# Self products of a block pair as seven partial products of 256 columns, and a run-end table from one-pass products, in a two-layer graph network kernel

## The chip, the cores and the metric

The kernel runs on one core of a Trainium2 chip. The metric is the device time of one execution in microseconds (us); the times given are of single executions and their median. A profile is one execution recorded by the hardware profiler. TensorE's records are called PE (matmuls) and PEld (weight loads), VectorE's DVE, ScalarE's ACT, GpSimd's POOL; SP is the engine that issues most plain DMAs.

## What is computed

There are 10,000 nodes with 512 features each and 160,000 edges, sorted by destination, each of one of four types.

```python
# layer 0, h = relu(layernorm(x))
h_all = einsum('nd,rdf->nrf', h, rel_W) + rel_b          # four relations
agg   = segment_sum(h_all[src, edge_type], dst) / max(deg, 1)
x1    = layernorm(h + h @ self_W + self_b + agg)
x     = x + layernorm(x1 + gelu(x1 @ W1 + b1) @ W2 + b2)
# layer 1, h = relu(layernorm(x)): twice
h     = relu(h @ W_self + (segment_sum(h[src], dst) / max(deg, 1)) @ W_neigh + b)
x     = x + h
```

All is fp32. The tables that say where each node's edges begin and end are made by the kernel too, from `dst`.

## The kernel before

**Two programs in one.** The first stage makes the table of messages (`hall_d`, 10,000 rows of four times 512) and the self terms (`xs_d`), and beside it the edge tables. Then three stages gather message rows and sum them per node, with the dense layers between. The first stage is ordered by a scheduler over the whole of it; the later stages stand in the order in which they are written. A branch between them takes a general program instead, where the edges do not fit the tables; it is not taken with these inputs.

**The table stage.** Nodes go in 78 blocks of 128 rows and a last one of 16. Blocks are taken in pairs (`sets`): first the block of 16, then 39 pairs. For a pair, `opened` normalises the rows, `turned` applies relu on ScalarE (`hg`, L641) and transposes each block by four products with the identity (`pT`, L172; copied out by ScalarE, L173). `mixed` (L651) forms four sums `s` of quarters of the transposed pair.

**Seven products for eight.** A pair of blocks by two halves of the contraction, times two relations' weights, is a 2 by 2 by 2 block product. The kernel forms it from seven products with sums before and after (the Winograd form). With `j` = 0 and 1 it does relations 0 and 2, then 1 and 3. Each of a half step's seven products (`times`, L724) is two matmuls of 128 by 128 by 512, into a PSUM tile `pm` from a pool of four buffers, `psM`. VectorE reads each with an addition (L731 to L748), and two additions in SBUF (L738, L739) finish the sums. Four stores per half step write `hall_d` from SP.

**The self product.** `residual`, once per half step, adds `ln2b` to the block's input rows (L657) and forms one block's self product: four matmuls of 512 columns with `wself` (L664) into a `pm` tile, which VectorE reads with the bias into `hg` (L666). `wself` has the identity added at the start (L682), which is the `h +` of the reference. `stored` writes the pair to `xs_d` (and its input rows to `xr_d`). The 12 pairs with blocks 52 to 75 (`late`) form no self product here: they store the transposed rows in `hT_d`, and a later stage does the product (L926). So 27 pairs and the block of 16 do it in the table stage.

**The edge tables.** `edges` is a generator; from the second pair on, each half step takes one of its steps with `next(step)`. `runs` finds the ends of the runs of equal destinations. Edges lie 1,250 to a partition; a key per run end holds its position, and twelve rounds of "eight largest, then strike them out" (L242, L245) take the ends out. Then, in twelve rounds of eight ends per partition, VectorE makes one-hot rows of the block (`inb`, L282) and of the lane (`inl`, L286), multiplies the latter by the edge number `end_f` (L289), and eight matmuls per round sum their products into one PSUM tile `pn` (L292): a table of the last edge number per node. What follows (L298 on) takes running maxima, degrees and offsets, on 79 partitions. `lists` then reads windows of the edge records (`win`, gathered by GpSimd) and makes the gather rows (`picked`, L468 to L491, and others). Both took their scratch from one pool `ep2` with two buffers a name.

**The start.** Weight differences (`mixes`, L704 to L707) are made by VectorE as the relation weights arrive. The small constants of the edge tables (L321 to L349) are put there too by the scheduler.

Of the kernel before, what the change touches and what calls it, by code (L numbers as in the profile page):

```python
# [21 lines left out]
def kernel(  # L22
# [152 lines left out]
    def runs(ep, ep2, pse, found):  # L175
# [15 lines left out]
        for p, n in ((0, P - 16), (P - 16, 15)):  # L191
# [11 lines left out]
        nc.gpsimd.iota(iota_j, pattern=[[1, EC]], base=1, channel_multiplier=0,  # L203
                       allow_small_or_imprecise_dtypes=True)
        base_e = ep.tile([P, 1], F32, name="base_e")
        nc.gpsimd.iota(base_e, pattern=[[0, 1]], base=0, channel_multiplier=EC,
                       allow_small_or_imprecise_dtypes=True)
        yield
        d_n = ep.tile([P, EC + 1], F32, name="d_n")
# [45 lines left out]
        n8 = ROUNDS * 8  # L255
        top_i = ep.tile([P, n8], I32, name="top_i")
        to_i = ep.tile([P, n8], I32, name="to_i")
        end_f = ep.tile([P, n8], F32, name="end_f")
        to_f = ep.tile([P, n8], F32, name="to_f")
        blk_f = ep.tile([P, n8], F32, name="blk_f")  # L260
        real = ep.tile([P, n8], F32, name="real")
        nc.vector.tensor_copy(top_i, top)
        nc.vector.tensor_scalar(to_i, top_i, 11, None, op0=OP.arith_shift_right)
        nc.vector.tensor_scalar(top_i, top_i, 2047, None, op0=OP.bitwise_and)
        nc.vector.tensor_copy(end_f, top_i)
        nc.vector.tensor_scalar(end_f, end_f, base_e, None, op0=OP.add)
        nc.vector.tensor_scalar(real, top, 0.0, sound, op0=OP.is_gt, op1=OP.mult)
        nc.vector.tensor_tensor(end_f, end_f, real, op=OP.mult)
        nc.vector.tensor_scalar(to_f, to_i, d_f[:, 0:1], None, op0=OP.add)
        nc.vector.tensor_copy(to_i, to_f)  # L270
        nc.vector.tensor_scalar(top_i, to_i, 7, None, op0=OP.arith_shift_right)
# [7 lines left out]
        for i in range(ROUNDS):  # L279
            w = slice(8 * i, 8 * i + 8)  # L280
            inb = ep2.tile([P, 8, NB], F32, name="inb")
            nc.vector.tensor_tensor(inb, lane[:, None, :NB].to_broadcast([P, 8, NB]),  # L282
                                    blk_f[:, w].unsqueeze(2).to_broadcast([P, 8, NB]),
                                    op=OP.is_equal)
            inl = ep2.tile([P, 8, P], F32, name="inl")
            nc.vector.tensor_tensor(inl, lane[:, None, :].to_broadcast([P, 8, P]),  # L286
                                    to_f[:, w].unsqueeze(2).to_broadcast([P, 8, P]),
                                    op=OP.is_equal)
            nc.vector.tensor_tensor(inl, inl, end_f[:, w].unsqueeze(2).to_broadcast([P, 8, P]),  # L289
                                    op=OP.mult)  # L290
            for j in range(8):
                nc.tensor.matmul(pn[:NB, :P], inb[:, j, :], inl[:, j, :], start=(i + j == 0),  # L292
                                 stop=(i == ROUNDS - 1 and j == 7))
            if i % 2:
                yield

        eb = ep.tile([NB, P], F32, name="eb")
        nc.vector.tensor_copy(eb, pn[:NB, :P])  # L298
        run = ep.tile([NB, P], F32, name="run")
        nc.vector.tensor_tensor_scan(run, eb, eb, 0.0, op0=OP.max, op1=OP.max)  # L300
        pr = pse.tile([P, 512], F32, name="pe")
# [278 lines left out]
            look_up(*ahead.pop(0))  # L580
            yield

    def edges(ep, ep2, pse):
        found = {k: ep.tile([P, NB], F32, name=f"f_{k}") 
                 for k in ["first", "deg", "from", "upto"] + [
                     f"{k}{lv}" for lv in range(NL) for k in ("sfrom", "supto", "sbase")]}
        with ExitStack() as s:
            yield from runs(s.enter_context(tc.tile_pool(name="er", bufs=1)), ep2, pse, found)
        with ExitStack() as s:
            yield from lists(s.enter_context(tc.tile_pool(name="el", bufs=1)), ep2, pse, found)  # L590


    with ExitStack() as s:
# [5 lines left out]
        psM = s.enter_context(tc.tile_pool(name="psM", bufs=4, space=PSUM))  # L599

        ep = s.enter_context(tc.tile_pool(name="ep", bufs=1))
        ep2 = s.enter_context(tc.tile_pool(name="ep2", bufs=2))
        step = edges(ep, ep2, pse)
        KH = KC // 2
        RH = R // 2
        sets = groups[len(groups) - (N % P > 0):] + [
# [22 lines left out]
        def opened(i):  # L629

            b0, nb, r = sets[i]
            xg = xgs.pop(i)
            sc = norm_scales(ap_, [xg[:r, c, :] for c in range(nb)], r, "a")
            return xg, sc, xp.tile([P, 2, D], F32, name="hg"), ap_.tile([P, 2, KC, P], F32,
                                                                       name="hT")
# [9 lines left out]
        def mixed(hT):  # L645

            s_ = [ap_.tile([P, KH, P], F32, name=f"s{i}", bufs=1) for i in range(4)]
            a11, a12, a21, a22 = hT[:, 0, :KH], hT[:, 0, KH:], hT[:, 1, :KH], hT[:, 1, KH:]
            for o, p, q, op in ((0, a21, a22, OP.add), (1, s_[0], a11, OP.subtract),
                                (3, a12, s_[1], OP.subtract), (2, a11, a21, OP.subtract)):  # L650
                nc.vector.tensor_tensor(s_[o], p, q, op=op)  # L651
            return a11, a12, a22, *s_

        def residual(rows, r, c, b):
            xg, _, hg, hT = rows
            h = hg[:r, c, :]
            nc.vector.tensor_tensor(xg[:r, c, :], xg[:r, c, :], ln2b[:r], op=OP.add)  # L657
            if b in late:
                i = late.index(b)
                nc.sync.dma_start(hT_d[i * P:(i + 1) * P, :], hT[:, c].rearrange("p k n -> p (k n)"))  # L660
                return
            pm = psM.tile([P, D], F32, name="pm")
            for k in range(KC):
                nc.tensor.matmul(pm[:r], rows[3][:, c, k, :r], wself[:, k, :], start=(k == 0),  # L664
                                 stop=(k == KC - 1))
            nc.vector.tensor_tensor(h, pm[:r], bself[:r], op=OP.add)  # L666
# [33 lines left out]
        for j in range(RH):  # L700
            b11, b21 = wrel[j][:, :KH], wrel[j][:, KH:]
            b12, b22 = wrel[j + RH][:, :KH], wrel[j + RH][:, KH:]
            t1, t2, t4 = (wp.tile([P, KH, D], F32, name=f"mix{j}_{i}") for i in range(3))
            nc.vector.tensor_tensor(t1, b12, b11, op=OP.subtract)  # L704
            nc.vector.tensor_tensor(t2, b22, t1, op=OP.subtract)
            nc.vector.tensor_tensor(t4, b21, t2, op=OP.subtract)
            nc.vector.tensor_tensor(b12, b22, b12, op=OP.subtract)  # L707
            mixes.append((b11, b21, b22, t1, t2, b12, t4))
        rows = opened(1)
        for c in range(2):  # L710
            turned(1, rows, c)
        for i, g in enumerate(sets):
            if g[2] < P:
                continue
            b0, nb, _ = g
            later = i + 1 if i + 1 < len(sets) else None
            if later:
                xgs[later] = load(sets[later])
            a11, a12, a22, s1, s2, s3, s4 = mixed(rows[3])

            def times(a, w):
                pm = psM.tile([P, D], F32, name="pm")
                for k in range(KH):
                    nc.tensor.matmul(pm, a[:, k, :], w[:, k, :], start=(k == 0),  # L724
                                     stop=(k == KH - 1))
                return pm

            for j in range(RH):
                b11, b21, b22, t1, t2, t3, t4 = mixes[j]
                p1, u2, p5, u3 = (ap_.tile([P, D], F32, name=n) for n in ("p1", "u2", "p5", "u3"))  # L730
                nc.vector.tensor_tensor(p1, times(a11, b11), bias(j), op=OP.add)  # L731
                nc.vector.tensor_tensor(u2, times(s2, t2), p1, op=OP.add)
                nc.vector.tensor_tensor(p5, times(s1, t1), bias(j + RH), op=OP.add)
                nc.vector.tensor_tensor(u3, times(s3, t3), u2, op=OP.add)
                gate[:] = [u3[:, :1]]
                nc.vector.tensor_tensor(p1, times(a12, b21), p1, op=OP.add)
                message(b0, j, p1)
                nc.vector.tensor_tensor(u2, p5, u2, op=OP.add)  # L738
                nc.vector.tensor_tensor(p5, p5, u3, op=OP.add)  # L739
                message(b0 + 1, j + RH, p5)  # L740
                if j == 0 and later:
                    rows_next = opened(later)
                if later:
                    residual(rows, P, j, b0 + j)
                    turned(later, rows_next, j)
                nc.vector.tensor_tensor(u3, times(a22, t4), u3, op=OP.add)
                message(b0 + 1, j, u3)
                nc.vector.tensor_tensor(u2, times(s4, b22), u2, op=OP.add)  # L748
                message(b0, j + RH, u2)
                if i > 1:  # L750
                    next(step, None)
            if not later:
                for c in range(2):
                    residual(rows, P, c, b0 + c)
            stored(g, rows)
            if later:
                rows = rows_next
# [789 lines left out]
```

## Time and profile before

| | us |
|---|---|
| runs shown | 6247.69, 6250.86, 6256.69 |
| median | 6250.86 |
| profiled execution | 6253.56 |
| its span | 6251.8 |

| engine | busy us | share of the span |
|---|---|---|
| PE | 5699.4 | 91% |
| PEld | 2517.3 | 40% |
| DVE | 3597.1 | 58% |
| ACT | 1858.2 | 30% |
| POOL | 3762.9 | 60% |

Shares of the whole span are means over stages with different limits, so the stage has to be looked at by itself: the table stage ends at about 1,236 us. The page gives the span in 40 slices of 156 us, each digit the busy share in tenths. Further views give busy time in stretches of chosen length, the chain of work that ended last (each piece followed back to what released it), and groups of equal instructions with their count, mean duration and the idle time before them. A fp32 matmul shows as two records. [...]

### The profile page before, as it was taken

What the parts mean: (1) busy time and instruction counts of PE and PEld (TensorE: products, weight loads), DVE (VectorE), ACT (ScalarE), POOL (GpSimd) and SP (SyncE); (2) the same over time, 40 slices, a digit from 0 to 9 for tenths busy, and PEclk for the clock granted to TensorE, in tenths of its full rate; (3) what the DMA queues carried; (4) which work ended last, traced back from release to release, by engine and by line L of the source; (5) the groups of instructions that cost most, each with busy time, mean ns of one, the idle gap of its engine ahead of it and who ended that gap; (6) DMA issues with size and microseconds to landing.
All of it is one profiled execution on the core that took longest, in us unless ns stands there. A gap on an engine that the chain in (4) does not pass through costs nothing.

```text
span 6251.8 us, 54551 instructions
## 1 busy us (share of the span) xinstructions
PE 5699.4 (91%) x14875; PEld 2517.3 (40%) x14875; DVE 3597.1 (58%) x7253; ACT 1858.2 (30%) x3672; POOL 3762.9 (60%) x3927
## 2 busy tenths in 40 slices
PE   9999999989999999999788888888879888888888
PEld 3444444444444444444333333333333333333333
DVE  8768889557777777776344444344334444444444
ACT  1016565013333333333322222222222222222221
POOL 0001110057777777775477777777767777777776
PEclk9999999989999999999899999999999999999999
DMA  4333344387887878886577777777778788878877
GB/s 162 114 117 118 122 136 154 132 275 243 255 256 242 256 246 252 256 257 196 187 234 237 237 234 237 237 234 237 237 232 251 249 247 251 250 246 251 250 246 217
DMA packets 503498, 1373.74 MB, mean 220 GB/s; under 512 B 82206, under 2 KB 82206, under 8 KB 503054
## 3 DMA queue, kind: packets, MB, share of 16 engines
q0 software_dynamic: 308768, 1008.91, 54.0%
q1 hardware_dynamic: 193886, 360.20, 15.9%
q8 instruction: 120, 1.97, 0.1%
q14 instruction: 196, 1.61, 0.1%
q10 hardware_dynamic: 528, 1.05, 0.1%
HBM read 1156.54 MB, written 213.30 MB: 219 GB/s over the span
## 4 chain that ended last, share of the span: by engine, by line
DMA 40%; PE 39%; DVE 8%; issue 7%; POOL 5%; ACT 1%; POOLq 0%; SPq 0%; DVEq 0%; ACTq 0%
DMA rows<-h_d,row 19%; PE pm L724 15%; DMA rows<-h_d,orow 14%; PE pa L847 6%; POOL rows L794 5%; PE ph L975 5%; PE po L986 4%; DVE pa L858 4%; DMA rows<-hall_d,row 4%; PE pm L664 3%; PE po L1218 1%; PE po L926 1%; DVE st L1013 1%; PE pT L172 1%; DMA tail<-h_d,srow 1%
## 5 line engine op out<-in xcount | busy, mean ns | idle before, releaser
L858 DVE TENSOR_TENSOR pa<-pa,rows 128x512 f32<-128x512 f32 x2574 | 1799.3, 699 | 2061.3 <-PE pa L847 1241.3
L794 POOL DMA_INDIRECT rows<-h_d,row x1716 | 1622.2, 945 | 522.7 <-issue 291.2
L847 PE MATMUL pa<-rows,hot 128*128 128x512 f32 (+1 forms) x2358 | 1247.7, 644 | 371.4 <-DMA rows<-h_d,orow 314.2
L794 POOL DMA_INDIRECT rows<-hall_d,row x858 | 868.1, 1012 | 273.6 <-issue 109.0
L794 POOL DMA_INDIRECT rows<-h_d,orow x786 | 743.1, 945 | 354.4 <-DMA h_d<-h 99.0
L847 PEld LDWEIGHTS pa<-rows,hot 128*128 128x128 f32 (+1 forms) x2358 | 407.1, 194 | 1151.9 <-DMA rows<-h_d,orow 829.0
L794 POOL DMA_INDIRECT rows<-hall_d,orow x393 | 378.2, 962 | 346.0 <-DVE hg L666 202.2
L986 PE MATMUL po<-w2s,hid 128*128 128x512 f32 (+1 forms) x1264 | 566.6, 602 | 17.2 <-DVE rest L1042 14.0
L1218 PE MATMUL po<-wss,hTb 128*128 128x512 f32 (+1 forms) x1264 | 579.7, 602 | 0.0
L1189 PE MATMUL po<-wns,mTb 128*128 128x512 f32 (+1 forms) x1264 | 573.5, 597 | 1.4 <-ACT mTb L173 1.4
L975 PE MATMUL ph<-x1T,w1s 128*128 128x512 f32 (+2 forms) x1344 | 558.7, 568 | 4.8 <-ACT hid L977 4.8
L173 ACT COPY mTb<-pT 128x512 f32<-128x512 f32 (+1 forms) x158 | 91.8, 581 | 1233.5 <-PE pT L172 1233.5
L1214 ACT ACTIVATE mb<-pa,rdeg 128x512 f32<-128x512 f32 (+1 forms) x158 | 108.5, 687 | 1130.0 <-DVE pa L858 1127.8
L829 PE MATMUL pa<-wss,ident 128*128 128x512 f32 x936 | 427.5, 593 | 0.0
L508 POOL DMA_INDIRECT win<-rec_d,at x79 | 76.0, 962 | 545.9 <-PE pe L533 364.8
L1189 PEld LDWEIGHTS po<-wns,mTb 128*128 128x128 f32 (+1 forms) x1264 | 240.2, 190 | 308.4 <-issue 272.4
L975 PEld LDWEIGHTS ph<-x1T,w1s 128*128 128x128 f32 x1344 | 249.4, 192 | 282.0 <-issue 273.4
L986 PEld LDWEIGHTS po<-w2s,hid 128*128 128x128 f32 (+1 forms) x1264 | 237.6, 191 | 308.2 <-issue 283.4
L847 PE MATMUL pa<-tail,hot 128*128 128x512 f32 x624 | 308.1, 611 | 50.6 <-DMA tail<-h_d,srow 47.1
L816 ACT ACTIVATE hot<-lane,loc 128x128 f32<-128x128 f32 x1098 | 337.7, 391 | 0.0
L1218 PEld LDWEIGHTS po<-wss,hTb 128*128 128x128 f32 (+1 forms) x1264 | 233.5, 195 | 235.3 <-issue 234.9
L724 PE MATMUL pm<-wrel,hT 128*128 128x512 f32 x624 | 296.5, 597 | 0.0
(289 smaller groups left out, 6224.5 us busy)
## 6 DMA issues: line engine op xcount, KB each, us to landing
hall_d<-p SPq DMA_DIRECT2D x156, 256.0 KB, 2.5
hall_d<-u SPq DMA_DIRECT2D x156, 256.0 KB, 2.4
hb<-h_d SPq DMA_DIRECT2D x156, 256.0 KB, 4.3
rows<-h_d,row POOLq DMA_INDIRECT x1716, 3.8
xg<-in_x_dram SPq DMA_DIRECT2D x39, 512.0 KB, 3.6
xr_d<-xg SPq DMA_DIRECT2D x39, 512.0 KB, 3.0
xs<-xs_d SPq DMA_DIRECT2D x39, 512.0 KB, 7.6
h_d<-h SPq DMA_DIRECT2D x39, 512.0 KB, 4.5
```

The costliest lines, as they stand in the source:

```text
L664: nc.tensor.matmul(pm[:r], rows[3][:, c, k, :r], wself[:, k, :], start=(k == 0), stop=(k == KC - 1))
L724: nc.tensor.matmul(pm, a[:, k, :], w[:, k, :], start=(k == 0), stop=(k == KH - 1))
L794: nc.gpsimd.indirect_dma_start(out=t[:n], out_offset=None, in_=table, in_offset=bass.IndirectOffsetOnAxis(ap=idx, axis=0))
L816: nc.scalar.activation(hot[:, t, :], lane, AF.Abs, bias=loc[:, b, t:t + 1], scale=-1.0)
L829: nc.tensor.matmul(p, ident, w, start=True, stop=True)
L847: nc.tensor.matmul(pa[:r], h, v, start=(i == 0), stop=(i == len(work) - 1))
L858: nc.vector.tensor_tensor(pa[:r], pa[:r], t[:r], op=OP.add)
L975: nc.tensor.matmul(ph[:, :n], w1s[:, k, f * P:(f + 1) * P], self.xT[:, k, :n], start=(k == 0), stop=(k == KC - 1))
L986: nc.tensor.matmul(po[:r], self.hid[:, f, c * r:(c + 1) * r], w2s[:, f, :], start=(f == 0), stop=(f == FC - 1))
L1189: nc.tensor.matmul(po[:r], mT[:, k, :r], wns[:, k, :], start=False, stop=(k == KC - 1))
L1214: nc.scalar.activation(m[:r], pa[:r], AF.Copy, scale=rdeg[:r, b:b + 1])
L1218: nc.tensor.matmul(po[:r], hT[:, k, :r], wss[:, k, :], start=(k == 0), stop=False)
```

## The change

The self products of a pair are formed like the relation products: a 2 by 2 by 2 block product over the pair's two blocks, two halves of the contraction and the two halves of 256 columns of `wself`. The sums `s` of the transposed pair, which are there already, serve again. The weight differences are made once, at the start (`halves`). The first four products are formed where block 0's self product stood, the other three where block 1's stood. The sums are kept in `hg`. Pairs in `late` and the block of 16 are as before.

In the run-end table, `end_f` holds two numbers per end: the position in its partition (1 to 1,250) and the partition's number, where one number held the partition times 1,250 plus the position. Both are multiplied with the one-hot lane row (`both`, one buffer), and one matmul of 256 columns in the reduced fp32 kind (`F32R`) sums both tables. VectorE puts them together afterwards. `inl` has one buffer, and the two halves of the edge work have scratch pools of their own.

```diff
@@ base_e
-        nc.gpsimd.iota(base_e, pattern=[[0, 1]], base=0, channel_multiplier=EC,
+        nc.gpsimd.iota(base_e, pattern=[[0, 1]], base=0, channel_multiplier=1,
...
-        end_f = ep.tile([P, n8], F32, name="end_f")
+        end_f = ep.tile([P, n8, 2], F32, name="end_f")
...
-        nc.vector.tensor_copy(end_f, top_i)
-        nc.vector.tensor_scalar(end_f, end_f, base_e, None, op0=OP.add)
+        nc.vector.tensor_copy(end_f[:, :, 0], top_i)
         nc.vector.tensor_scalar(real, top, 0.0, sound, op0=OP.is_gt, op1=OP.mult)
-        nc.vector.tensor_tensor(end_f, end_f, real, op=OP.mult)
+        nc.vector.tensor_tensor(end_f[:, :, 0], end_f[:, :, 0], real, op=OP.mult)
+        nc.vector.tensor_scalar(end_f[:, :, 1], real, base_e, None, op0=OP.mult)
@@ for i in range(ROUNDS)
-            nc.vector.tensor_tensor(inb, lane[:, None, :NB].to_broadcast([P, 8, NB]),
+            nc.vector.tensor_tensor(inb.bitcast(F32R), lane[:, None, :NB].to_broadcast([P, 8, NB]),
...
-            inl = ep2.tile([P, 8, P], F32, name="inl")
+            inl = ep2.tile([P, 8, P], F32, name="inl", bufs=1)
...
-            nc.vector.tensor_tensor(inl, inl, end_f[:, w].unsqueeze(2).to_broadcast([P, 8, P]),
+            both = ep2.tile([P, 8, 2, P], F32, name="both", bufs=1)
+            nc.vector.tensor_tensor(both.bitcast(F32R),
+                                    inl[:, :, None, :].to_broadcast([P, 8, 2, P]),
+                                    end_f[:, w].unsqueeze(3).to_broadcast([P, 8, 2, P]),
                                     op=OP.mult)
             for j in range(8):
-                nc.tensor.matmul(pn[:NB, :P], inb[:, j, :], inl[:, j, :], start=(i + j == 0),
-                                 stop=(i == ROUNDS - 1 and j == 7))
+                nc.tensor.matmul(pn[:NB, :2 * P], inb[:, j, :].bitcast(F32R),
+                                 both[:, j].rearrange("p o n -> p (o n)").bitcast(F32R),
+                                 start=(i + j == 0), stop=(i == ROUNDS - 1 and j == 7))
...
         nc.vector.tensor_copy(eb, pn[:NB, :P])
+        nc.vector.scalar_tensor_tensor(eb, pn[:NB, P:2 * P], float(EC), eb, op0=OP.mult, op1=OP.add)
@@ edges: scratch pools er2 and el2 in place of ep2
...
+        def halves():
+            bias1, bias2 = bself[:, :D // 2], bself[:, D // 2:]
+            b11, b12, b21, b22 = (wself[:, k:k + KH, n:n + D // 2]
+                                  for k in (0, KH) for n in (0, D // 2))
+            t1, t2, t3, t4 = (wp.tile([P, KH, D // 2], F32, name=f"half{i}") for i in range(4))
+            for t, p, q in ((t1, b12, b11), (t2, b22, t1), (t4, b21, t2), (t3, b22, b12)):
+                nc.vector.tensor_tensor(t, p, q, op=OP.subtract)
+
+            def parts(rows, terms):
+                a11, a12, a22, s1, s2, s3, s4 = terms
+                hg = rows[2]
+                left, right = (hg[:, :, n:n + D // 2] for n in (0, D // 2))
+
+                def plus(out, a, w, v):
+                    pm = psM.tile([P, D], F32, name="pm")[:, :D // 2]
+                    for k in range(KH):
+                        nc.tensor.matmul(pm, a[:, k, :], w[:, k, :], start=(k == 0),
+                                         stop=(k == KH - 1))
+                    nc.vector.tensor_tensor(out, pm, v, op=OP.add)
+
+                def first():
+                    plus(left[:, 0], a11, b11, bias1)
+                    plus(right[:, 0], s2, t2, left[:, 0])
+                    plus(right[:, 1], s1, t1, bias2)
+                    plus(left[:, 1], s3, t3, right[:, 0])
+
+                def second():
+                    plus(left[:, 0], a12, b21, left[:, 0])
+                    nc.vector.tensor_tensor(right[:, 0], right[:, 1], right[:, 0], op=OP.add)
+                    nc.vector.tensor_tensor(right[:, 1], right[:, 1], left[:, 1], op=OP.add)
+                    plus(left[:, 1], a22, t4, left[:, 1])
+                    plus(right[:, 0], s4, b22, right[:, 0])
+
+                return first, second
+            return parts
+
-        def residual(rows, r, c, b):
+        def residual(rows, r, c, b, terms=None):
...
+            if terms:
+                self_parts(rows, terms)[c]()
+                return
             pm = psM.tile([P, D], F32, name="pm")
```

In the changed file the products of `plus` are at L678 and its additions at L680, the two SBUF additions at L690 and L691, the weight differences at L667, the product `both` at L290 and its matmuls at L295; the relation products of L724 are at L774, and the additions of L731 to L748 at L781 to L798.

More of the change, by code (lines that the diff above doesn't have):

```diff
@@ L257, in runs @@
         to_i = ep.tile([P, n8], I32, name="to_i")
-        end_f = ep.tile([P, n8], F32, name="end_f")
+        end_f = ep.tile([P, n8, 2], F32, name="end_f")
         to_f = ep.tile([P, n8], F32, name="to_f")
         blk_f = ep.tile([P, n8], F32, name="blk_f")
-        real = ep.tile([P, n8], F32, name="real")
+        real = top
         nc.vector.tensor_copy(top_i, top)
@@ L581, in lists, with edges @@
             yield
-    def edges(ep, ep2, pse):
+    def edges(ep, pse):
         found = {k: ep.tile([P, NB], F32, name=f"f_{k}")
@@ L587, in edges @@
         with ExitStack() as s:
-            yield from runs(s.enter_context(tc.tile_pool(name="er", bufs=1)), ep2, pse, found)
+            er2 = s.enter_context(tc.tile_pool(name="er2", bufs=2))
+            yield from runs(s.enter_context(tc.tile_pool(name="er", bufs=1)), er2, pse, found)
         with ExitStack() as s:
-            yield from lists(s.enter_context(tc.tile_pool(name="el", bufs=1)), ep2, pse, found)
+            el2 = s.enter_context(tc.tile_pool(name="el2", bufs=2))
+            yield from lists(s.enter_context(tc.tile_pool(name="el", bufs=1)), el2, pse, found)
     with ExitStack() as s:
@@ L601 @@
         ep = s.enter_context(tc.tile_pool(name="ep", bufs=1))
-        ep2 = s.enter_context(tc.tile_pool(name="ep2", bufs=2))
-        step = edges(ep, ep2, pse)
+        step = edges(ep, pse)
         KH = KC // 2
@@ L708 @@
             mixes.append((b11, b21, b22, t1, t2, b12, t4))
+        self_parts = halves()
         rows = opened(1)
@@ L718 @@
                 xgs[later] = load(sets[later])
-            a11, a12, a22, s1, s2, s3, s4 = mixed(rows[3])
+            terms = mixed(rows[3])
+            a11, a12, a22, s1, s2, s3, s4 = terms
             def times(a, w):
@@ L743 @@
                 if later:
-                    residual(rows, P, j, b0 + j)
+                    residual(rows, P, j, b0 + j, terms)
                     turned(later, rows_next, j)
@@ L753 @@
                 for c in range(2):
-                    residual(rows, P, c, b0 + c)
+                    residual(rows, P, c, b0 + c, terms)
             stored(g, rows)
```

## The prediction

> **What bounds the kernel now.** I read the page's slices first, then the table stage by the stretches of 25 us, the chain of waits inside it, and the groups with their shapes. Both edits lie in that stage, the first 1,236 us; what follows it is issued in the same order in both programs on every engine, so it can only start earlier or later.
>
> ```profile
> PE   9999999989999999999788888888879888888888
> DVE  8768889557777777776344444344334444444444
> ```
>
> Slices of 156 us: in the first eight TensorE is full and VectorE close behind. The stretches (PE, PEld, DVE, ACT, POOL, then the clock, DMA share and GB/s) say how close, part by part:
>
> ```profile
> 100.00:125.00 25.00, 25.00 (x66) 11.47 (x65) 25.00 (x36) 4.36 (x4) 0.00 (x0) 1.00 0.34 125
> 200.00:225.00 25.00, 25.00 (x65) 11.42 (x64) 13.53 (x26) 2.99 (x5) 0.00 (x0) 1.00 0.28 104
> 550.00:575.00 25.00, 25.00 (x84) 11.71 (x81) 23.54 (x104) 18.00 (x39) 3.82 (x4) 1.00 0.31 104
> ```
>
> TensorE is never idle, at full clock; VectorE is full where the largest keys are picked (100), half used with no table work (200), 94% used in the list building (550). The chain (start, duration) is TensorE alone:
>
> ```profile
> 107.08 12.02 PE pm L724 x28
> 119.09 3.43 PE pm L664 x8
> 122.97 12.02 PE pm L724 x28
> ...
> 253.96 3.50 PE pe L292 x32
> 257.45 8.59 PE pm L724 x20
> ```
>
> A half step (one j of a pair of blocks) is 15.89 us: 12.02 for seven relation products, 3.43 for one block's self product, 0.44 for four transposes. An fp32 matmul of 512 columns is two records, 0.429 us each. In six half steps (254 to 354) 32 records of L292 add 3.50, making 19.39. So a microsecond of TensorE removed here is a microsecond of the end, as long as VectorE keeps up.
>
> The groups that price the change (count, busy us, mean ns, then idle before):
>
> ```profile
> L664 PE MATMUL pm<-wself,hT 128*128 128x512 f32 x416 | 187.0, 592 | 0.0
> L666 DVE TENSOR_TENSOR hg<-pm,bself 128x512 f32<-128x512 f32 x52 | 35.8, 688 | 42.4 <-PE pm L664 42.3
> L651 DVE TENSOR_TENSOR s<-hT 128x256 f32<-128x256 f32 x76 | 29.2, 420 | 6.9 <-ACT hT L173 6.5
> L292 PE MATMUL pe<-inl,inb 128*79 128x128 f32 x192 | 21.9, 273 | 0.0
> L289 DVE TENSOR_TENSOR inl<-inl,end_f 128x1024 f32<-128x1024 f32 x12 | 14.6, 1216 | 0.0
> ```
>
> A matmul's mean overlaps its neighbours; what it costs is the spacing of starts. VectorE's overlap too: independent 512-column adds start 0.60 us apart, 256-column ones 0.33.
>
> **What the Trainium skill says.** "TensorE: Matmul & The Clock Gate", Back-to-back issue gap, gives 518 cycles for 512 columns and 262 for 256: halving the columns costs some 6 cycles per pass. The trace has no 256-column product, but L292's 128-column records, two passes each, start 0.109 us apart, 0.003 over the columns' own time, the same as 512's. "FP8 and Floating Point Precision", TensorE Precision Notes: true fp32 takes four passes, the reduced kind reads the same four-byte words and cuts them short. The trace agrees, and shows that the reduced kind takes one pass: 0.859 us for 512 fp32 columns, 0.23 for the reduced products of the next stage:
>
> ```profile
> 1293.12 0.39 PE L847 MATMUL pa<-lower,hot 128*128 128x512 f32 x1
> 1293.35 0.40 PE L847 MATMUL pa<-upper,hot 128*128 128x512 f32 x1
> 1293.58 0.40 PE L847 MATMUL pa<-lower,hot 128*128 128x512 f32 x1
> ```
>
> "VectorE: DVE Perf Modes", The TRN2 errata: an fp32 two-tensor operation takes (N+151)/0.96 ns; 424, 691 and 1224 for 256, 512 and 1024, where the trace has 420, 688 and 1216. I use 2.29 for 2,048, which the trace lacks.
>
> **The change, part by part.**
>
> Self products. 27 pairs form them (26 early, and the last). Before: 16 records of 0.429 = 6.87 us per pair. After: 7 products of two matmuls of 256 columns, 28 records of 0.2133 + 0.003 = 6.05. Saved 0.82 per pair, **22.1 us** over 27 pairs (lowest 21, were a record 0.22; highest 22.9). Weight loads (190 ns) still fit under 0.216, with 0.026 to spare.
>
> VectorE in exchange: two 512-column adds go (1.20), seven 256-column sums from PSUM and two in SBUF come (nine at 0.33, or 0.42 when dependent: 3.0 to 3.8). Per half step +0.9 to +1.3. No part of this is on the chain while VectorE has room. Without table work it has 8.6 of 15.89 (13.53 of 25). In list building the mean of the stretches from 500 to 900 is 21.3 of 25, 14.0 per 16.45 us half step; after, 14.9 to 15.3 against TensorE's 16.0. In picking the largest keys it is full, 15.9 per half step; the changed program's order spreads those twelve rounds over seven half steps instead of five, which leaves some 15 against TensorE's 15.5. I take **+2 us** for stalls in both (0 to 8).
>
> The four PSUM buffers of pm: a product can start when the one four before it has been read. The small ones last 0.86, so three cover 2.6 us instead of 5.2. What is late next is the read by L736 (L786 in the new file) for the fourth small product:
>
> ```profile
> 573.62 1.88 PE L724 MATMUL pm<-wrel,hT 128*128 128x512 f32 x4
> ...
> 575.98 0.68 DVE L736 TENSOR_TENSOR p<-pm,p 128x512 f32<-128x512 f32 x1
> ```
>
> There the fifth product ends at 575.3 and is read by 576.7; the fourth small one would start at 577.9. It has 1.2 us of slack behind one of VectorE's longest bursts.
>
> The run-end table. Before, 96 fp32 matmuls of 128 columns, 192 records of 0.109 = 21.0 us. After, 96 one-pass ones of 256 columns: 0.107 of columns and the 0.017 that the 512-column ones show above theirs, 0.125 each, 12.0 us. If weight loads set the pace (0.149 for 79 columns of L292 to 0.19) it is up to 18.2; at best 10.5. VectorE instead multiplies 2,048 elements per round for 1,024: 2.2 for 1.14 between starts. A half step of this section then asks of VectorE 8.6 + 0.9 + 2 x (0.73 + 1.14 + 2.2) = 17.7, and of TensorE 12.02 + 0.44 + 3.02 + 2.0 = 17.5. They are level, where TensorE stood alone before. The product tile `both` has one buffer: each multiplication waits for the eight matmuls of the round before, with the next half step's L731 (L781) and all evictions queued behind it; TensorE has four tiles ahead, and in the new order the next eight sit one and a half relation products later, 2.6 us, about the time the multiplication takes. I take 18.0 per half step for 19.39: **8.3 us** over six (with three pairs' self saving in it). Bounds: 17.5 with no wait (11.3 saved), 19.4 (nothing saved) if every round shows 0.9 us of wait.
>
> The small operations (table indices, one more 79-row operation after the sum) move by under 1 us of VectorE: nothing, covered by TensorE.
>
> The start. Four subtractions of 512 columns (0.60 each) make the weight differences. VectorE idles from 8.9 to 13.5 waiting for relation weights, which hides three. The fourth, and some 1.4 us of constants that fell into that idle time before, move behind 13.5, and there TensorE does wait:
>
> ```profile
> 32.52 3.70 PE L724 MATMUL pm<-mix,s 128*128 128x512 f32 x8 [1.82 <-DVE s L651]
> ```
>
> VectorE has 0.46 of slack up to there: **+1.5 us** (0 to 2.5).
>
> The handover. The last pair's blocks are now complete only after the seventh product, so gathers that were released by the first block's eviction (1232.4) come nearer the end; the chain there goes through the reload of hT_d after the second block. **+0.5** (0 to 2).
>
> DMAs: none added, the store of xs_d waits for the seventh sum instead of L666; ScalarE's next hg (467.8) stands 12 us ahead of its transposes (480.3), which covers it. Pools: the two halves of the table work get scratch of their own in turn; the later one already waited for the earlier.
>
> Sum: 24 pairs outside the section 24 x 0.82 = -19.7; section -8.3; stalls +2; start +1.5; handover +0.5: **-24.0 us**. The profiled execution was 6253.56 (span 6251.8), 2.7 above the median 6250.86. From the median: **6227**.
>
> **Rivals.**
>
> *VectorE holds part of it (0.17).* For: 25.00 of 25 at 100 us, level loads in the section. Against: 54% at 200. The section saves nothing (+8.3), and picking and list building lose 6 more, as at the upper bound: -24 + 14 = -10, some 6241.
>
> *Small PSUM windows turn into stalls: slower (0.09).* Place: the second to fourth small product of each pair, behind a VectorE burst. Price: each us of read delay beyond the 1.2 of slack stops TensorE, 27 times. It decides from a mean stall of 0.9 us per pair (24/27), which eats all; 2 us gives +54 - 24 = +30, 6281. Against: the slack above is from a heavy burst, and the extra VectorE work before that point is a third of a microsecond per sum.
>
> *The one-pass product does not run as one.* Weight loads at 0.19 add 6 us, so -18, 6233: inside the first case. If both edits and covers come out at their best, -33, 6218.
>
> **How the numbers follow.** A measurement of this kernel can tell about 0.2%, 12.5 us, from no change. The main case (0.74) runs from -33 to -13 with -24 the likeliest. The second case is mostly within 12.5 us. Range 6217 to 6245: the best case below, the second case above, the slower one left out. Faster 0.77, same 0.14, slower 0.09.
>
> **What would show it.** Right: in the changed profile the chain of the table stage is still TensorE; half steps near 15.9 and 15.1 alternately for four and three small products; the section near 18.0; the next stage's first self products (L926 before, at 1242.2) near 1218. Wrong: idle time of TensorE before the 256-column products put down to L784 or L786; one-pass records over 0.15 us apart; VectorE full over hundreds of us while TensorE has gaps; a first relation product later than by 2.5 us.

## The result and the profile after

| | before | after |
|---|---|---|
| median of six runs, us | 6250.33 | 6228.53 |
| lowest to highest | 6247.69 to 6256.69 | 6223.69 to 6230.92 |
| profiled execution | 6253.56 | 6229.31 |
| its span | 6251.8 | 6227.6 |

The ratio of after to before is 0.996, with a 95% interval of 0.9949 to 0.997: 21.8 us less by the medians, 24.2 by the spans. The forecast was 24.0 less, 6227. The sum came out; four of its terms did not, and the rest of this text is mostly about those.

The slices of the page, TensorE and VectorE, of after:

```profile
PE   9999999899999999999788888888879888888888
DVE  8889999457777777776333434434434444444444
```

The table stage ends in the eighth slice. TensorE is as full as before up to there, with less to do, and its 8 has moved from the ninth slice to the eighth with the end of the stage; VectorE's digits are higher in five of the first seven and equal in the other two, and 9 from the fourth to the seventh.

The stretches of after, for two of the times shown of before (PE, PEld, DVE, ACT, POOL, clock, DMA share, GB/s):

```profile
100.00:125.00 25.00, 25.00 (x78) 13.89 (x78) 25.00 (x37) 3.64 (x3) 0.00 (x0) 1.00 0.26 100
200.00:225.00 25.00, 25.00 (x78) 13.76 (x77) 16.88 (x36) 2.99 (x5) 0.00 (x0) 1.00 0.28 109
```

With no table work beside it (200) VectorE went from 13.53 to 16.88 of 25. Where the largest keys are picked (100) it is at 25.00, as before, and still TensorE loses nothing: 25.00 of 25. A full engine is not yet an engine that somebody waits for.

The chain of waits in the table stage of after (start, duration, work), first outside the section (the six half steps that hold the products of the run-end table), then at its beginning:

```profile
141.27 12.02 PE pm L774 x28
153.29 2.59 PE pm L678 x12
156.32 12.02 PE pm L774 x28
168.34 3.45 PE pm L678 x16
172.23 12.02 PE pm L774 x28
...
267.47 3.44 PE pm L774 x8
...
284.43 3.44 PE pm L774 x8
...
302.27 3.44 PE pm L774 x8
```

The chain is still TensorE's own work. Half steps are 15.05 and 15.91 apart by turns, the short one with the three small products (2.59) and the long one with the four (3.45), where all were 15.89. In the section (267 to 302) they are 16.96 and 17.84, where all were 19.39.

The groups of after that stand in the place of those shown of before (count, busy us, mean ns, idle before):

```profile
L678 PE MATMUL pm<-half,s 128*128 128x256 f32 x324 | 75.5, 382 | 2.1 <-DVE u L784 1.4 <-DVE p L786 0.7
L680 DVE TENSOR_TENSOR hg<-pm,hg 128x256 f32<-128x256 f32 x135 | 55.3, 416 | 12.0 <-PE pm L678 11.5
L290 DVE TENSOR_TENSOR both<-inl,end_f 128x2048 fp32r<-128x2048 f32 x12 | 27.4, 2287 | 1.0 <-PE pe L295 0.9
L295 PE MATMUL pe<-both,inb 128*79 128x256 f32 x96 | 16.1, 309 | 0.0
```

L290 waits for the eight products of the round before for 1.0 us in all twelve rounds together, so its single buffer hardly holds up VectorE, and TensorE nowhere. The multiplication of 2,048 elements takes 2287 ns; the trace of before lacked it, and the formula in the Trainium skill, "VectorE: DVE Perf Modes", The TRN2 errata, gives (2048+151)/0.96 = 2291. The first line shows the idle time of TensorE before the new products, 2.1 us, and both of its parts lie in the first pair. TensorE's timeline there, with the transposes and relation products that follow:

```profile
40.75 1.13 PE L678 MATMUL pm<-half,s 128*128 128x256 f32 x4
43.30 1.13 PE L678 MATMUL pm<-half,s 128*128 128x256 f32 x4 [1.41 <-DVE u L784]
45.16 1.62 PE L678 MATMUL pm<-half,s 128*128 128x256 f32 x4 [0.73 <-DVE p L786]
46.57 1.06 PE L172 MATMUL pT<-ident,hg 128*128 128x128 f32 x4
47.42 2.71 PE L774 MATMUL pm<-mix,hT 128*128 128x512 f32 x4
```

And what holds VectorE at that time:

```profile
37.28 1.29 DVE L160 BATCH_NORM_STATS2 sta<-xg 128x6 f32<-128x512 f32 x2 [3.51 <-DMA xg<-in_x_dram]
```

VectorE's queue has the statistics of the next pair's rows ahead of the additions that read the PSUM buffers (L782 to L786). The rows land late, VectorE stands still for 3.51 us, and what lies behind it is late too. In the kernel before it stood there for 2.99 us, and TensorE did not feel it.

The last two lines of TensorE's timeline show a second loss. Four transposes take 1.06 us where they take 0.60 elsewhere, and the four records of a relation product 2.71 where they take 1.88. TensorE waits for nothing here; its granted clock (the number after the busy times) is at half:

```profile
45.70:49.00 3.30, 3.30 (x9) 2.08 (x8) 2.91 (x10) 0.88 (x2) 0.00 (x0) 0.50 0.49 173
```

The stretch at half clock lasts from 45.7 to 49.1, 3.4 us, and so costs 1.7. The table stage of before has none. It can't be seen in a mean: over the first 1,200 us the clock is 1.00 in both.

The starts of the transposes give the shift of every half step against before: +3.7 at the second half step, +4.0 at the third, then 0.82 less per pair; -11.9 over the section; -25.6 at the last half step. The +4.0 is made of 0.5 for relation products that start later (a wait of 2.30 for 1.82), 2.8 for the two waits with the longer first record after each, and 1.7 for the half clock, less the pair's own saving of 0.8 and 0.1 by which the pair starts earlier. One more wait stands at the start of the list building, 0.20 us before a relation product at 418.6, again put down to L786; with the longer record after it, it costs 0.5. The first product of the next stage (L926 before, L976 after) starts at 1216.10 for 1242.23, -26.1. GpSimd's first message gather, which belongs to that stage, moves by only 24.4, as these two lines of its timelines say, of before and of after:

```profile
1232.39 0.94 POOL L794 DMA_INDIRECT rows<-hall_d,orow  x1 [202.24 <-DVE hg L666]
```

```profile
1207.97 0.94 POOL L844 DMA_INDIRECT rows<-hall_d,orow  x1 [203.38 <-PE pm L678]
```

It was released by an addition of block 0's whole self product before, and by the last but one of the seven small products after.

### The profile page after: what moved, and what is told of

It reads as the page before. It is cut to its first block, busy times and chain, and to the rows that moved or that the text cites. A ratio compares the mean times of both kernels' runs of the same rounds, so it can differ in the third digit from the quotient of the medians.

```text
span 6227.6 us, 55230 instructions
## 1 busy us (share of the span) xinstructions
PE 5669.9 (91%) x15103; PEld 2565.6 (41%) x15103; DVE 3657.2 (59%) x7447; ACT 1858.6 (30%) x3672; POOL 3769.6 (61%) x3927
## 3 DMA queue, kind: packets, MB, share of 16 engines
q10 hardware_dynamic: 528, 1.05, 0.1%
## 4 chain that ended last, share of the span: by engine, by line
DMA 40%; PE 37%; DVE 9%; issue 7%; POOL 5%; ACT 2%; SPq 0%; POOLq 0%; DVEq 0%; ACTq 0%
DMA rows<-h_d,row 20%; PE pm L774 15%; DMA rows<-h_d,orow 13%; PE pa L897 6%; POOL rows L844 5%; DMA rows<-hall_d,row 5%; PE po L1036 4%; DVE pa L908 4%; PE ph L1025 4%; PE pm L678 2%; PE po L1268 1%; PE po L976 1%; DMA rows<-hall_d,orow 1%; DVE st L1063 1%; PE pT L172 1%
## 5 line engine op out<-in xcount | busy, mean ns | idle before, releaser
L774 PE MATMUL pm<-wrel,hT 128*128 128x512 f32 x624 | 296.5, 597 | 0.0
```

## The experiments

TensorE was granted 0.90 of its full clock over the span in the first four and the last three runs, and 0.98 in the others; in the first 1,200 us the mean clock was 1.00 in all, but seven of the thirteen profiles, that of the changed kernel among them, have one stretch of 3.4 us at half clock in the first 50 us, which costs up to 1.7 us. So the table stage is read from the traces, with that stretch in mind, and times only as ratios to the kernel before on the same chip. Kernels without a ratio were executed once. A shift is that of a half step's start, against the kernel before.

**Each half alone.** The first kernel has the new self products and the old table, the second the old self products and the new table.

```diff
# first (base_e, end_f and both go back with it)
-                nc.tensor.matmul(pn[:NB, :2 * P], inb[:, j, :].bitcast(F32R), both[:, j]...
+                nc.tensor.matmul(pn[:NB, :P], inb[:, j, :], inl[:, j, :], ...
# second (halves is not called)
-            if terms:
-                self_parts(rows, terms)[c]()
-                return
```

> Only the self products are changed; the run-end table is as before. If TensorE alone sets the table stage, each of 27 pairs saves 0.82 us (22.1) and the first pair loses the 4.1 us of waits seen at the start of the changed kernel: 18 us less than before, near 6232, with half steps 0.84 shorter by turns and 19.4 and 18.5 in the section with the table's matmuls. If the section's saving in the changed kernel needed both edits together, this one gives less than 16 us.

> Only the run-end table is changed; self products are as before. TensorE theory: 192 records of 0.109 us become 96 of 0.127, 21.0 us become 12.2, so 8.8 us less than before, near 6241.5, half steps of the section 17.9 for 19.39, and no wait in the first pair. If VectorE (8.6 + 8.2 = 16.8 us of work per half step, with waits for the single buffer) holds the section instead, half steps stay above 18.3 and less than 6 us is saved.

Measured: the self products alone shift every half step by -0.84 and +0.02 by turns, inside the section too, and the stage by -17.8; the first pair takes +2.2 net, with TensorE's idle time put down to L779 (1.3) and L781 (0.7), the lines that are L784 and L786 in the changed kernel. The table alone makes each of the section's half steps 17.82 and shifts the stage by -9.5; its first pair moves by 0.02. The ratios are 0.998 (0.9964 to 0.9995) and 0.9988 (0.9976 to 1.0).

The two stage shifts add up to -27.3, the whole change has -25.6. The difference of 1.7 lies in the first pair (4.0 for 2.2), and it is in the main the half clock: neither of these two runs has it in its table stage, and the waits are nearly the same (2.5 us with the longer records after them, for 2.8). The halves do not disturb each other: the stalls expected from both together, on a VectorE loaded by both, do not exist. The first pair's waits belong to the self products alone.

**The first pair whole.**

```diff
-                    residual(rows, P, j, b0 + j, terms)
+                    residual(rows, P, j, b0 + j, terms if i > 1 else None)
```

> The changed kernel, but the first pair forms its self products as before (four matmuls of 512 columns per block). If the waits at the start come from small products that give VectorE less time to read PSUM buffers, they go: 4.1 us back, 0.8 given up, 3.3 us less than the changed kernel, near 6225. If they come from VectorE being late there whatever follows, the wait stays and the time rises by 0.8.

Measured: no idle time is put down to L784 or L786 any more, the shift after the first pair is +0.46 for +4.0, and the stage ends 29.6 before the old one, 4.0 better than the changed kernel. That is 0.7 more than the 3.3 expected, and not for the reason given: 1.7 of it is the half clock, which this run's table stage does not have. Against the self products alone, which have small products in the first pair and no half clock either, whole ones are 1.7 better after that pair (+0.46 for +2.16): about 2.5 of waits less 0.84. The ratio is 0.9966 (0.9953 to 0.9979), too wide for 4 us. The 0.46 that remains is all that the constants and the fourth subtraction cost at the start.

**The wide table in true fp32.**

```diff
-                nc.tensor.matmul(pn[:NB, :2 * P], inb[:, j, :].bitcast(F32R),
-                                 both[:, j].rearrange("p o n -> p (o n)").bitcast(F32R),
+                nc.tensor.matmul(pn[:NB, :2 * P], inb[:, j, :],
+                                 both[:, j].rearrange("p o n -> p (o n)"),
```

> The changed kernel with the table's 256-column matmuls in full fp32 instead of the one-pass kind; nothing else differs. If the pass count is what makes the table cheaper, 96 matmuls of two records of 0.216 us take 41.5 us for 12.2, and the kernel is 29 us slower than the changed one, near 6258, with half steps of the section near 22.3. If VectorE set the section, much of that would be hidden and it would be under 20 us slower.

Measured: half steps of 22.85 and 21.99 in the section, 22.42 in the mean, 5.02 more than in the changed kernel; the stage ends 2.8 after the old one. The ratio is 0.9997 (0.9986 to 1.0009). The matmuls are now 192 records in place of 96. Sixteen products per half step are dearer by 5.02/16 = 0.314 each, so that one in true fp32 takes about 0.127 + 0.314 = 0.44 us (0.127 is the spacing shown below), and the reduced kind is what pays for the second column block. In true fp32 the section is 18.2 longer than the old one, with the self products' saving in it.

**One VectorE operation more, and eight products more.** The first adds VectorE's work to each half step of the section, the second TensorE's.

```diff
# first
+            if i % 2:
+                more = ep2.tile([P, 8, P], F32, name="inl", bufs=1)
+                nc.vector.tensor_tensor(more, lane..., to_f[:, w]..., op=OP.is_equal)
# second
+            if i % 2:
+                pd = pse.tile([P, 512], F32, name="pe")
+                for j in range(8):
+                    nc.tensor.matmul(pd[:NB, :2 * P], inb[:, j, :].bitcast(F32R),
+                                     both[:, j]....bitcast(F32R), start=True, stop=True)
```

> The changed kernel with one VectorE operation more in each of the six half steps of the table section (the comparison that fills inl, 1,024 columns, made once more in every second round; 1.22 us each by its row). It is read from the starts of the half steps. In the changed kernel those of the section are 17.83 and 16.97 apart, and VectorE is busy for 24.8 of 25 us there, though TensorE waits for it almost nowhere. Theory, both engines are full in the section: each half step becomes longer by 0.9 to 1.2, the section by 5.5 to 7.2, and TensorE's idle time named after VectorE's additions by as much. Rival, VectorE still has room, since the section lost exactly what TensorE's work lost: 0 to 1 in the whole section.

> The changed kernel with eight one-pass products of 256 columns more in each of the six half steps of the section, into PSUM that nothing reads: 8 x 0.127 = 1.02 us of TensorE's time each. Theory, TensorE sets the half step (its periods are its own work): 1.0 us more in each, 6.1 in the section, and VectorE's busy share in it falls by 6 in 100. Rival, VectorE sets it: 0 to 1 in the section, and TensorE's products are absorbed.

Measured against the changed kernel: with 7.3 us more of VectorE's work the section is not longer, but 0.14 shorter; eight products more lengthen each half step by 0.95 or 1.05, the section by 5.9 (and the start of the list building by 0.9). The six half steps of the section, of the changed kernel and of these two, in that order (PE, PEld, DVE, ...):

```profile
249.03:353.43 104.40, 104.40 (x373) 60.55 (x372) 99.03 (x151) 8.97 (x15) 0.00 (x0) 1.00 0.29 106
```

```profile
247.16:351.42 104.26, 104.26 (x373) 60.88 (x372) 101.42 (x146) 8.39 (x13) 0.00 (x0) 1.00 0.25 94
```

```profile
248.78:359.08 110.30, 110.30 (x422) 66.25 (x421) 100.08 (x151) 8.99 (x15) 0.00 (x0) 1.00 0.27 100
```

My theory that both engines set the half step fell. VectorE is busy for 99.03 of 104.40 us, 16.5 per half step of 17.40; TensorE waits in none of the three. The 24.8 of 25 that the theory was built on was the fullest 25 us of the section, not the section. TensorE alone sets the half step. But VectorE's room is small: with the extra operations it is at 101.42 of 104.26, and 3.1 us more of its work than in the changed kernel falls into the two half steps behind the section. Part of the extra work was put off, then, and what a longer section would do is not shown. With eight more products its share falls from 95 to 91 in 100, 4 for the 6 expected. The second kernel also gives the price of a one-pass product by its effect: 0.119 to 0.131.

**Three PSUM buffers, in the changed kernel and in the one before, and five.**

```diff
-        psM = s.enter_context(tc.tile_pool(name="psM", bufs=4, space=PSUM))
+        psM = s.enter_context(tc.tile_pool(name="psM", bufs=3, space=PSUM))   # 5 in the third, with pse 2 for 3
```

> The changed kernel with three PSUM buffers for the partial products in place of four. It sizes the room behind the rival that small windows turn into stalls. A 256 column product takes 0.87 us, so that with three buffers VectorE may be late by about 0.35 us before TensorE waits, with four by about 1.2. Theory, four buffers are the room that hid VectorE's long operations: plain half steps cost 0 to 0.1 more, the first pair's loss grows from 4.1 to about 5, and the section and the list building lose 5 to 15 in all. Rival, the windows do not matter, VectorE is on time everywhere but in the first pair: under 1 us in all beyond the first pair.

> The kernel before with three PSUM buffers for partial products in place of four. The changed kernel lost 4.35 by this, 0.74 of it in the first pair and the rest at the start of the key picking, at the start of the list building and in four of its later half steps. Theory, the small windows made that loss (each whole self product holds TensorE for 1.72, a partial one for 0.87): the kernel before loses under 1 in all. Rival, the relation products' windows made it: the kernel before loses 3 to 4.5 at the same places.

> The changed kernel with five PSUM buffers for partial products in place of four (the table's pool has two in place of three). Each more holds one small product of 0.87 us. Theory, the first pair stalls because the window is short while VectorE waits for a load: its loss of up to 4.1 falls by 0.8 to 1.8, everything else stays within 0.2. Rival, the loss is VectorE's lateness itself, which must be paid whatever the window: no change in the first pair against the changed kernel of the same call, within 0.3.

| shift, us | first pair, against before with four | half clock there | from there to the stage's end, against the same kernel with four | the whole stage, against the same kernel with four |
|---|---|---|---|---|
| changed, four | +4.0 (+4.3 in a second execution) | behind the waits | 0 | 0 |
| changed, three | +4.8 | behind the waits | +3.6 | +4.35 |
| changed, five | +1.5 | ahead of the small products | +1.0 | -1.6 |
| before, three | +2.1 | none | +1.1 | +3.2 |

Both expectations on three buffers missed: the changed kernel loses more than the rival's 1 and less than the theory's 5 beyond the first pair (3.6, at the start of the key picking and of the list building and in a few half steps later), and the kernel before loses 3.2, two thirds of it in the first pair, more than the theory's 1, and only 0.6 of it, at the start of the list building, at one of the rival's places. So beyond the first pair the short windows cost 3.6 where the long ones cost 1.1, and the first pair's wait reaches the old kernel too as soon as it has three buffers. With four, the changed kernel has just enough of them everywhere but in the first pair and at the start of the list building. With five, the first pair shows no idle time put down to L784 or L786. It is 2.8 better than in the changed kernel of the same chip, but most of that is not the buffers' doing, as the next paragraphs show. Nor did everything else stay within 0.2: the list building loses 1.0 against the changed kernel's first execution, 0.6 against its second. The table's PSUM pool gave up a buffer for the fifth, which may be why; that was not tried by itself.

The first pair's loss is not one number. Over the six executions with four buffers and small products there it was 2.0, 2.0, 2.2, 3.8, 4.0 and 4.3 (the whole change twice, and four kernels that differ from it only in the section). What divides them is the half clock. In the three high ones it comes at about 45, behind or within the waits, and adds up to 1.7. The one of 2.2 (self products alone) has none. In the two of 2.0 (the wide table in true fp32, and one VectorE operation more) it comes at about 33, ahead of the small products: TensorE loses the 1.7 there, VectorE catches up meanwhile, and of the waits only 0.4 and 0.6 are left. These are the runs that the one with five buffers can be set beside, since its stretch begins at 34. Eight records of relation products, some 6 us ahead of the small ones, of the changed kernel and of the run with five:

```profile
32.89 3.70 PE L774 MATMUL pm<-mix,s 128*128 128x512 f32 x8 [2.30 <-DVE s L657]
```

```profile
33.02 5.40 PE L774 MATMUL pm<-mix,s 128*128 128x512 f32 x8 [2.30 <-DVE s L657]
```

So the fifth buffer's gain in the first pair is 0.5 (+1.5 for +2.0), less than the theory's 0.8 to 1.8; it took away the 0.4 to 0.6 of waits that were left.

What brings the half clock on is not shown. Seven of the eight profiles with small products in the first pair have it, and none of the five with whole ones. But in three of the seven it begins (33 to 34 us) before the first small product (41.5 to 41.7). There it begins within 1 us of the end of a wait of 2.2 to 2.3 us, and seven other runs waited as long at that place and went on at full clock.

**Both ends whole, and the changed kernel again.**

```diff
-                    residual(rows, P, j, b0 + j, terms)
+                    residual(rows, P, j, b0 + j, terms if i > 1 else None)
...
-                    residual(rows, P, c, b0 + c, terms)
+                    residual(rows, P, c, b0 + c)
```

> The changed kernel with whole self products in the first pair (as in the run before, which took the wait of 3.2 us away) and in the last pair, too. Theory on the gathers: their first one waits for the next to last 256 column product of the last pair in the changed kernel, 2.2 us ahead of the last pair's hT_d load, and for the first whole product's addition in the kernel before, 4.5 us ahead of it; as the gathers then go on at 1.25 us each until the stage ends, that start sets the end. So here: the hT_d load comes 0.8 later than with the first pair alone whole, and the first gather 1.4 earlier. Rival, the gathers wait for something that moves with the last product: both 0.8 later. For the time: 1.4 us less than with the first pair alone whole, 6222 against 6228.5 of the changed kernel on a chip like that of the first runs; the share is 0.9955 to 0.9965 of before on any.

> The changed kernel once more, beside the next two. By its two engines' own work nothing in the table stage moves but the first pair, whose loss hangs on when a load lands: 2 to 4.1 against the kernel before. If the gathers set the end, the time from the start of the first gather to the end of the span is that of the four runs before on this kind of chip (5025.6 to 5029.9), and the share is 0.995 to 0.9965 of before.

Measured, both ends whole: the last half step starts 3.7 before the changed kernel's (1.7 of it the half clock, which this run lacks in its table stage), the next stage's first product only 2.7 before it, but the first gather 4.9 before it. Set against the 3.7, the gathers are 1.2 earlier and the products 1.0 later (1.4 and 0.8 were expected), and the releaser is the one of before, the addition of a whole self product (L714 in this file):

```profile
1203.07 0.94 POOL L844 DMA_INDIRECT rows<-hall_d,orow  x1 [202.18 <-DVE hg L714]
```

So what the gathers wait for is settled: with whole products in the last pair they start at the first block's addition, with partial ones at the last pair's last but one product. The ratios are 0.9956 (0.9942 to 0.9969) and, for the changed kernel again, 0.9958 (0.9946 to 0.9971). The version whose gathers start first, 4.9 us ahead, cannot be told from the changed kernel by these times: 5 us are 0.08%. The changed kernel's first pair took +4.3 in its second execution, just above the expected 2 to 4.1. Its start-to-end time can't be set beside the other four: its chip ran the later stages slower.

Whether the gathers' start or the first product sets the end of the next stage was to come out of this too, and did not. From the first gather to the last of that stage it takes 1695.0 us in the kernel before, 1694.4 in the changed one, and 1693.5 to 1696.7 in the four other runs at that clock; from the first product to that last gather it is 1685.2, 1686.3, and 1684.4 to 1688.5. Both are about as constant.

## Why the prediction was right, and where its terms were wrong

The sum was -24.0 and the span moved by -24.2. By terms:

| term | predicted | measured | from |
|---|---|---|---|
| pairs outside the section, but for the first | -18.9 (23 x 0.82) | -18.9 | 0.82 per pair |
| the section | -8.3 | -11.9 | half steps 17.40, not 18.0 |
| the first pair: start and its own saving | +0.7 (1.5 - 0.82) | +4.0 | shift after the first pair: start 0.5, waits 2.8, half clock 1.7, saving -0.8, earlier start -0.1 |
| stalls in key picking and list building | +2 | +0.5 | one wait, at 418.6 |
| handover | +0.5 | +2.3 | -26.7 at the reload of hT_d, -24.4 at the gathers |

*Self products: right to the hundredth.* A 256-column fp32 record costs 0.216 us, as worked out from the columns' own time plus 0.003, and 28 of them for 16 of 0.429 are 0.82 a pair. The gap that the Trainium skill gives ("TensorE: Matmul & The Clock Gate", Back-to-back issue gap) puts it at 262 cycles per pass, by estimate 218 ns for two at its 2.4 GHz; the trace agrees within 2. Weight loads, 190 ns by their records, did not stand in the way.

*The section: the step that was mis-sized is VectorE's demand.* I worked out 17.7 per half step for VectorE and 17.5 for TensorE, called them level, and added waits up to 18.0. The profile after shows VectorE at 16.5 and no such wait, and the run with one operation more shows that a further 1.22 per half step does not lengthen the section. TensorE's side was right: 17.40 for 17.5, with one-pass products 0.127 apart (0.125 estimated). These two lines of the timeline of after give the mean spacing, eight products between the two starts, (257.41 - 256.39)/8; the first of the eight takes 0.184, the others about 0.118:

```profile
256.39 1.18 PE L295 MATMUL pe<-both,inb 128*79 128x256 f32 x8
257.41 2.74 PE L774 MATMUL pm<-mix,s 128*128 128x512 f32 x6
```

The bound of 17.5 with no wait was the answer; that one pass is what the reduced kind takes ("FP8 and Floating Point Precision", TensorE Precision Notes, has four for true fp32) is borne out by the fp32 version, 3.5 times as dear.

*The stalls: 0.5.* The mechanism of the first rival, VectorE holding part of the gain, was priced at +2 in the main case. VectorE is at 373 of 400 us from 500 to 900, and at 25.00 of 25 in the key picking, and TensorE idles in neither; the one wait stands between them, at 418.6. That three buffers cost 3.6 us in just these places shows that it was the fourth that hid VectorE's lateness, and how little was to spare.

*The first pair: the cause I gave was the small one.* I blamed constants and a fourth subtraction (1.5). They cost 0.46, by the runs with that pair whole; the wait that I pointed to (1.82 before L724) grew to 2.30. The waits, 2.5 to 2.8 us, are the mechanism of the slower rival, in one pair out of 27: small products whose PSUM buffers are read late. It was sized from a burst of VectorE's own work, with 1.2 us of slack. What came was a wait for a DMA at the head of VectorE's queue, 3.5 us. The trace of before had that wait (2.99), and I had not asked what would be late behind it once the windows were halved. The sign that the prediction named for this, idle time before the 256-column products put down to L784 or L786, is in the profile, 2.1 us of it. The remaining 1.7 is the half clock, of which the prediction knew nothing: it took TensorE to be at full clock through the stage, as it was in the trace of before.

*The handover: right mechanism, just past its range.* 0 to 2 was given, 0.5 taken, 2.3 found at the start of the gathers. Whether it reaches the span is argued, not shown: the stage that follows keeps -26.6 at a product around 2,873 us of after and -25.1 at its last ones, where VectorE waits for the last gathers to land, and those are issued 25.1 earlier; the span moved by 24.2. Runs that separate the two starts by 2 us could not tell them apart at the end.

So two terms that were priced too dear, by 3.6 and 1.5, stood against two that were too cheap, by 3.3 and 1.8, and 1.7 of the 3.3 is a stretch at half clock that other profiles here do not have. So the number came out in part by luck; it was better than its working.

## What to carry to other kernels

When products become smaller, each PSUM buffer hides less of the reader's lateness: look for the longest wait in the reading engine's queue, DMA waits at its head above all, and set it against what the buffers hold in time, place by place and at the start of the pipeline too. Two engines that look level in one stretch need not be: add a known piece of work to each and see which of the two moves the end. A mean clock of 1.00 can hide a stretch at half clock: where two traces part at one place, compare the spacing of equal records there before giving it a cause. And where the last items of a stage release another engine's first ones, the form that is quickest in the middle need not be the one to use for the first and the last item.

## What the hardware showed that I had not expected

- One-pass products of 256 columns start 0.118 us apart within a group of eight (0.127 in the mean of the group shown above, whose first one is longer), though their weight loads (128 x 79) last 0.147 us by their own records; the loads overlap one another, so that the length of a load's record is not what sets the pace. The excess over the columns' own time (107 ns, half of what the two passes of a 256-column fp32 record show, less 1.5) is 11 ns, where each pass of a true fp32 product shows 1.5. The gap of 262 cycles cited above (by estimate 109 ns) holds for a pass of the true fp32 product here, and not for the one-pass one.
- TensorE's granted clock fell to half for 3.4 us once in the first 50 us, in seven of thirteen profiles, and took up to 1.7 us each time. Where it came ahead of the small products, the waits for VectorE shrank from 2.1 us (after) to 0.4 and 0.6.
- The same program took 6229 us on one chip and 7069 on another. Its table stage was the same within 0.7 us, at full clock in both but for the 3.4 us named above; from 1,200 to 6,200 us the granted clock was 0.88 for 0.97, and the DMA rate 208 GB/s for 242. Why was not tried.
